# Message passing over sorted edges: the order of VectorE's register loads, the addresses of the sums, and 114 columns a chunk in place of 104

## The chip, the cores and the metric

The kernel runs on one core of a Trainium2 chip. The metric is the device time of one execution in microseconds. The kernel before took 4946.85 us, the median of three runs (4942.31 to 4949.29). The engines are named as the profile names them: PE is TensorE (PEld its weight loads), DVE VectorE, ACT ScalarE, POOL GpSimd, SP SyncE, which here only issues DMAs.

## What is computed

One layer of a graph network, over N = 12,500 nodes of 48 features and E = 400,000 edges of 32 features, with a hidden size of 128. The edges are sorted by `dst`; `src` is random.

```python
edge_index = jnp.stack([src, dst])
h = jnp.maximum(_layernorm(x, axis=-1), 0.0)
# in the layer, on h:
x_i = x[dst]
x_j = x[src]
tmp = jnp.concatenate([x_i, x_j, edge_attr], axis=1)
h = jax.nn.relu(tmp @ W1 + b1)
msg = h @ W2 + b2
out = jax.ops.segment_sum(msg, dst, num_segments=N_NODES)
# and last: x + out
```

## The kernel before

**Two stages.** `node_tables` (from L85) computes the layer norm and two tables in DRAM, one row of 128 numbers for each node: `tab_b` (h times the rows of W1 that meet `src`), and `tab_a` (h times the rows that meet `dst`, plus b1). After it the kernel asks whether the edges' windows fit (a flag), and for these data runs `windows` (from L204), which is nearly all of the time. The other branch, `general`, isn't run.

**A chunk.** `windows` goes over 391 chunks of 1024 edges, in 8 tiles of 128. Since `dst` is sorted, the edges of a chunk meet at most 80 neighbouring nodes (`W = 80`). For a chunk, these steps follow each other, each on its engine:

- SP loads 13 numbers into its registers and issues the loads of `rhs` (the chunk's 80 rows of `tab_a`, L347), of `lhs`'s edge features (L349) and of `row` (the chunk's `dst`, L351).
- POOL gathers the rows of `tab_b` for the chunk's tiles, one indirect DMA for each tile of 128 edges (L358), into one of six buffers `gb`. So the gathers of chunk c wait until the hid add of chunk c − 6 has read its buffer.
- DVE makes `lhs`'s one-hot part from `row` (L366, which also gives the degrees `deg`) and the one-hot matrix `hot` (L372).
- PE multiplies `lhs` with `rhs` into `pre` (L384); DVE adds the gathered rows, `hid = pre + gb` (L403; called the hid add here); ACT takes the relu (L408).
- PE multiplies the hidden rows with `hot`, which sums over the edges of each node (L416), and the degrees by an identity matrix (L419), into `p_g`; DVE adds `p_g` to a running sum `seg`, at a place that the chunk's first node gives (L426; the seg add).

Every 12 chunks the sums are multiplied with W2 (L452, L453), added to x (L454) and stored (L458); while it awaits that, SP issues nothing else. Then the other of two `seg` buffers is cleared and begun (L442, L444).

**Tiles without a gather.** For some chunks one of the eight tiles isn't gathered by POOL. For 305 of them (`BYCOLS`), its 128 source rows are collected as columns: `tab_b` lies transposed in SBUF too (`bt`, 128 x 12,544), and DVE and ACT copy one column after another into a tile `gt` (L339), which PE transposes into `pre` (L394); its relu is a small one of ACT (L407). For 36 others (`BYROWS`), SP loads row after row from DRAM, 12 a chunk (`gs`, L292). Each column's number has to be in a register of the engine that copies it. `load` (with `numbers`) loads the registers of one part by one instruction, `columns` makes the copies. `PARTS` says, for each part, whether it is DVE's, its first column, its length, and where its numbers lie in the table `last`:

```python
PARTS = ((True, 0, 27, 1), (True, 27, 17, 28), (False, 44, 28, 48), (False, 72, 32, 76))
PART = sum(n for _, _, n, _ in PARTS)
```

So 104 columns are copied in each chunk, 44 by DVE and 60 by ACT, whichever tile they belong to; a longer list of columns a chunk gives more tiles by columns (`tiles_of`) and so fewer gathers.

**What sets the order.** The order on each engine is the order of the code (`manual_schedule`). The loop's iteration c does the early steps of chunk c, PE's and the hid add of chunk c − 1, and the seg add of chunk c − 2. On DVE an iteration is: lhs (L366), load of part 1, hot (L372), columns of parts 0 and 1, the hid add of c − 1 (L403), the seg add of c − 2 (L426), load of the next chunk's part 0. On ACT it is: columns of part 2, relu of c − 1, columns of part 3. The place of the seg add and the row of `rhs` are numbers of a node, from which a register calculation makes the address; a column's number is already an address, since it is made in advance, for the whole table `last`, by a multiplication with 4 and an offset of `BT0`, the address at which `bt` lies.

**The start.** The three tiles `deg` are cleared by POOL (L251) inside `windows`, behind a pool's storage that `node_tables` used; so POOL's first gather, which is behind them on its engine, waits as well.

Of the kernel before, what the change touches and what calls it, by code (L numbers as in the profile page):

```python
# [8 lines left out]
F32 = mybir.dt.float32  # L9
I32 = mybir.dt.int32  # L10
AF = mybir.ActivationFunctionType
ALU = mybir.AluOpType
# [4 lines left out]
P = 128  # L17
N, D, DE, HID, E = 12500, 48, 32, 128, 400000
# [6 lines left out]
NCH = (NT + T - 1) // T  # L25
W = 80
# [4 lines left out]
L = 1024  # L31
FAR = L - W
# [11 lines left out]
U8 = mybir.dt.uint8  # L44
# [6 lines left out]
ROWS0 = 3  # L51
END = NT // T

PARTS = ((True, 0, 27, 1), (True, 27, 17, 28), (False, 44, 28, 48), (False, 72, 32, 76))
PART = sum(n for _, _, n, _ in PARTS)
BASE = 108
RPART = 12

BT0 = 16512


SEG, NEXT, SEG2 = 122, 123, 124
WIDTH = 128
SLOTS = (NCH + 2 + P - 1) // P
MOST = 32

# [137 lines left out]
def windows(nc, tc, gp, bt, ident, idx, x_t, tab_a, tab_b, dst, edge_t, w1, w2s, b2s, out_t):  # L204


    srci, rel, bw, wrow, last = idx
    with ExitStack() as es:
        one = es.enter_context(tc.tile_pool(name="wone", bufs=1))
        ld = es.enter_context(tc.tile_pool(name="ld", bufs=3))  # L210
        gtp = es.enter_context(tc.tile_pool(name="gtp", bufs=3))
# [18 lines left out]
        rows_at = slice(BASE + 1, BASE + 1 + RPART)  # L230
# [3 lines left out]
        tab8 = tab_b.rearrange("n h -> (n h)").bitcast(U8)  # L234

        place = PARTS[0][3] - 1
        for a, b in ((place, SEG2), (NEXT, SEG)):
# [5 lines left out]
        segs = []  # L243
        for k in range(2):
            seg = one.tile([P, 2, L], F32, name=f"seg{k}")
            nc.vector.memset(seg, 0.0)
            segs.append(seg)
        degs = []
        for k in range(3):
            deg = one.tile([W, P], F32, name=f"deg{k}")  # L250
            nc.gpsimd.memset(deg, 0.0)  # L251
            degs.append(deg)

        rhss = []
        for k in range(3):
            rhs = one.tile([P, HID], F32, name=f"rhs{k}")
            nc.sync.dma_start(rhs[W:K, :], w1[2 * D :, :])
            rhss.append(rhs)
        st = {}
        gts = {}  # L260
        gss = {}

        def group(c):

            return divmod(c + OFF, GQ)
# [15 lines left out]
        def node(n):  # L281
            return n.with_bounds(min_val=0, max_val=N - 1)
# [34 lines left out]
        def load(c, part):  # L317

            dve, first, n, at = PARTS[part]
            n = max(0, min(n, len(BYCOLS) * P - ((c - COLS) * PART + first))) if c >= COLS else 0  # L320
            engine = mybir.EngineType.DVE if dve else mybir.EngineType.Activation
            if part == 0 and 2 <= c < NCH + 2:
                base, *nodes = numbers(c, at - 1, n + 1, engine)
                st[c - 2]["base"] = base.with_bounds(min_val=0, max_val=FAR)
            else:
                nodes = numbers(c, at, n, engine) if n else []
            regs[c, part] = nodes

        def columns(c, part):

            dve, first, _, _ = PARTS[part]
            copy = nc.vector.tensor_copy if dve else nc.scalar.copy
            for k, at in enumerate(regs.pop((c, part), [])):
                j, e = divmod((c - COLS) * PART + first + k, P)
                of = BYCOLS[j]
                if of not in gts:
                    gts[of] = gtp.tile([HID, P], F32, name="gt")
                at = at.with_bounds(min_val=BT0, max_val=BT0 + 4 * (N - 1)) - BT0
                copy(gts[of].bitcast(U8)[:, 4 * e : 4 * e + 4], bt8[:, bass.ds(at, 4)])  # L339

        def prepare(c):
            n = min(T, NT - c * T)
            at = c * CE
            m = max(0, min(RPART, len(BYROWS) * P - (c - ROWS0) * RPART)) if c >= ROWS0 else 0
            base, *nodes = numbers(c, BASE, 1 + m, mybir.EngineType.SP)
            rhs = rhss[c % 3]
            nc.sync.dma_start(rhs[:W, :], tab_a[bass.ds(node(base), W), :])  # L347
            lhs = ld.tile([P, CE], F32, name="lhs")
            nc.sync.dma_start(lhs[W:K, : n * P], edge_t[:, at : at + n * P])  # L349
            row = ld.tile([W, CE], I16, name="row")  # L350
            nc.sync.dma_start(  # L351
                row[:, : n * P],
                dst[at : at + n * P].rearrange("(o e) -> o e", o=1).to_broadcast([W, n * P]),
            )
            st[c] = dict(n=n, rows=nodes)
            gb = gp.tile([P, T, HID], F32, name="gb")
            for t in range(n - (c in BYCOLS) - (c in BYROWS)):
                nc.gpsimd.indirect_dma_start(  # L358
                    out=gb[:, t, :], out_offset=None, in_=tab_b[:, :],
                    in_offset=bass.IndirectOffsetOnAxis(  # L360
                        ap=srci[:, c * T + t : c * T + t + 1], axis=0
                    ),
                )

            deg = degs[c % 3]
            nc.vector.tensor_scalar(  # L366
                lhs[:W, : n * P], row[:, : n * P], bw[:, c : c + 1], None,
                op0=ALU.is_equal, op1=ALU.add, accum_out=deg[:, :1],
            )
            load(c, 1)  # L370
            hot = wp.tile([P, T, W], F32, name="hot")
            nc.vector.tensor_tensor(  # L372
                hot[:, :n, :], wnum.unsqueeze(1).to_broadcast([P, n, W]),
                rel[:, c * T : c * T + n].unsqueeze(2).to_broadcast([P, n, W]), op=ALU.is_equal,
            )
            st[c].update(rhs=rhs, lhs=lhs, gb=gb, deg=deg, hot=hot)

        def before(c):
# [43 lines left out]
        def add(c):  # L422

            s = st.pop(c)
            to = segs[group(c)[0] % 2][:, :, bass.ds(s["base"], W)]
            nc.vector.tensor_add(to, to, s["p_g"])  # L426

        xs = {}
# [31 lines left out]
        with tc.manual_schedule():  # L460
            for c in range(NCH + 2):
                if c < NCH:
                    prepare(c)
                    if c < BUILD:
                        part = turn_load(c)
                    rows(c, st[c].pop("rows"))
                columns(c, 0)
                columns(c, 1)
                if 0 <= c - 1 < NCH:
                    before(c - 1)  # L470
                if 0 <= c - 2 < NCH:
                    fold(c - 2)
                if 0 <= c - 1 < NCH:
                    turned(c - 1)

                g, k = group(c - 2)
                if k == GQ - 3 or c == NCH - 1:
                    segment_load(g)
                if g > 0 and k < L // BLK:
                    segment_sum(g - 1, k, BLK)  # L480
                if g > 0 and k == STORE:
                    segment_store(g - 1, L)
                columns(c, 2)
# [145 lines left out]
def tile_gnn_preln(  # L629
# [43 lines left out]
    wrow = const.tile([P, W], F32, name="wrow")  # L673
# [85 lines left out]
    outside = nc.values_load(flag[:1, :1], min_val=0, max_val=1)  # L759

    with tc.If(outside == 0) as cmp:
        windows(nc, tc, gp, bt, ident, (srci, rel, bw, wrow, last), x_t, tab_a, tab_b, dst16, edge_t,
                w1, w2s, b2s, out_t)
    with cmp.Else():
        general(nc, tc, bt, ident, x_t, tab_a, tab_b, src_it, dst_it, dst, edge_t, w1, w2s, b2s,
# [71 lines left out]
```

## Time and profile before

| | |
|---|---|
| median of three runs | 4946.85 us (4942.31 to 4949.29) |
| the profiled execution | 4948.09 us, its span 4946.4 us |
| mean granted TensorE clock | 0.607 of full speed |
| busy, share of the span | PE 65%, PEld 58%, DVE 59%, ACT 58%, POOL 54% |
| instructions | 92,158 in all, DVE 18,764, ACT 23,270, POOL 2,812 |
| gathers on POOL (L358) | 2,784, busy 2654.2 us |
| column copies (L339) | DVE 16,540, ACT 22,500 |
| HBM over the span | 73 GB/s |

Times are microseconds of one profiled execution. A row of the costliest groups names line, engine, operation, output and inputs with their shapes and the number of instructions, then after the bar the busy time and the mean of one in ns, and after the next bar the engine's idle time just before these instructions with what ended most of it. "issue" stands for time in which the engine waited for nothing that the profile shows. A row of a timeline has its start, its length from first start to last end, engine, line, operation and how many equal ones follow each other, and in brackets the idle time ahead. Register loads, branches and DMA-issuing instructions don't count as busy. The slices of the page show that from 250 us on the kernel is even: each fortieth of the span looks like the next.

### The profile page before, as it was taken

How to read it: one execution, taken by the hardware profiler on the slowest of the kernel's cores; microseconds unless marked ns; L12 is line 12 of the kernel's file. 1: busy time of each engine (PE TensorE's matmuls, PEld its weight loads, DVE VectorE, ACT ScalarE, POOL GpSimd, SP SyncE). 2: the span in 40 equal slices, each digit the busy share in tenths (PEclk: the TensorE clock that was granted, in tenths of full speed). 3: DMA queues.
4: the chain of work that ended last, by engine and by line, in shares of the span. 5: the costliest groups of instructions: out<-in, count | busy, mean ns of one | idle time of the engine just before them, and what ended most of it. 6: DMA issues, size and time to landing. Idle time of an engine off the chain costs nothing. (4 is left out here: it accounts for less than half of the span.)

```text
span 4946.4 us, 92158 instructions
## 1 busy us (share of the span) xinstructions
PE 3197.2 (65%) x14504; PEld 2884.0 (58%) x14504; DVE 2942.6 (59%) x18764; ACT 2864.2 (58%) x23270; POOL 2675.9 (54%) x2812
## 2 busy tenths in 40 slices
PE   4565666666666666666666666666666666666666
PEld 3555556555555555656555555655666555555656
DVE  3255666666666666566666666666566666666665
ACT  2146666666566666566656566666566666566665
POOL 5555555555555555555555555555555555555552
PEclk7665655566666565556565666555555665666555
DMA  5422222222222222222222222222222222222221
GB/s 208 111 78 71 70 70 67 68 70 72 70 70 68 67 70 71 70 70 69 66 70 71 70 70 68 67 70 70 70 70 68 68 69 71 70 69 69 70 67 51
DMA packets 214695, 363.63 MB, mean 74 GB/s; under 512 B 70419, under 2 KB 119717, under 8 KB 212805
## 3 DMA queue, kind: packets, MB, share of 16 engines
q0 software_dynamic: 89120, 182.66, 14.4%
q1 hardware_dynamic: 124704, 174.89, 11.8%
q14 instruction: 491, 4.01, 0.3%
q8 instruction: 120, 1.97, 0.2%
q10 hardware_dynamic: 260, 0.10, 0.0%
HBM read 337.91 MB, written 22.07 MB: 73 GB/s over the span
## 5 line engine op out<-in xcount | busy, mean ns | idle before, releaser
L358 POOL DMA_INDIRECT gb<-tab_b,srci x2784 | 2654.2, 953 | 2167.6 <-DVE seg L426 1273.1
L339 ACT COPY gt<-bt 128x4 uint8 x22500 | 2421.0, 189 | 1761.1 <-issue 1734.7
L339 DVE COPY gt<-bt 128x4 uint8 x16540 | 1516.0, 193 | 1464.2 <-issue 1457.9
L416 PE MATMUL p_g<-hot,hid 128*128 128x80 f32 x6250 | 1368.2, 407 | 1557.6 <-ACT hid L408 1446.3
L416 PEld LDWEIGHTS p_g<-hot,hid 128*128 128x128 f32 x6250 | 1291.5, 314 | 1648.2 <-ACT hid L408 1528.5
L384 PEld LDWEIGHTS pre<-rhs,lhs 112*128 112x128 f32 x6250 | 1254.8, 306 | 140.1 <-issue 95.7
L384 PE MATMUL pre<-rhs,lhs 112*128 112x128 f32 x6250 | 1291.4, 393 | 52.1 <-DVE hid L403 38.8
L366 DVE TENSOR_SCALAR_CACHE_REDUCE lhs<-row,bw 80x1024 f32<-80x1024 int16 x391 | 498.1, 1274 | 253.5 <-issue 181.1
L403 DVE TENSOR_TENSOR hid<-pre,gb 128x896 f32<-128x896 f32 (+2 forms) x391 | 429.7, 1099 | 67.5 <-remote 53.8
L408 ACT ACTIVATE hid<-hid 128x896 f32<-128x896 f32 (+1 forms) x391 | 376.1, 962 | 120.4 <-DVE hid L403 91.1
L372 DVE TENSOR_TENSOR hot<-wnum,rel 128x640 f32<-128x640 f32 x391 | 322.0, 823 | 95.7 <-issue 95.7
L394 PE MATMUL pre<-ident,gt 128*128 128x128 f32 x610 | 220.0, 464 | 93.6 <-remote 49.8
L419 PE MATMUL p_g<-ident,deg 80*128 80x80 f32 x782 | 237.4, 405 | 2.7 <-issue 2.7
L394 PEld LDWEIGHTS pre<-ident,gt 128*128 128x128 f32 x610 | 164.0, 328 | 101.3 <-remote 53.6
L419 PEld LDWEIGHTS p_g<-ident,deg 80*128 80x128 f32 x782 | 203.4, 317 | 2.7 <-issue 2.7
L426 DVE TENSOR_TENSOR seg<-seg,p_g 128x160 f32 x391 | 120.9, 309 | 51.3 <-issue 23.4
L452 PE MATMUL p_f<-seg,w2s 128*48 128x512 f32 (+1 forms) x134 | 121.9, 1010 | 0.4 <-DVE seg L426 0.4
L407 ACT ACTIVATE hid<-pre 128x128 f32<-128x128 f32 x305 | 81.9, 268 | 60.8 <-DVE hid L403 51.7
L453 PE MATMUL p_f<-seg,b2s 1*48 1x512 f32 (+1 forms) x134 | 111.2, 924 | 0.0
L453 PEld LDWEIGHTS p_f<-seg,b2s 1*48 1x48 f32 x134 | 14.5, 159 | 102.0 <-issue 102.0
L311 ACT COPY bt<-pre 128x1024 f32<-128x1024 f32 (+1 forms) x13 | 12.4, 957 | 94.7 <-remote 71.5
L454 DVE TENSOR_TENSOR xseg<-xseg,p_f 48x512 f32<-48x512 f32 (+1 forms) x67 | 45.0, 671 | 29.7 <-PE p_f L453 22.5
(65 smaller groups left out, 348.7 us busy)
## 6 DMA issues: line engine op xcount, KB each, us to landing
gs<-tab_b SPq DMA_DIRECT2D x4608, 0.5 KB
row<-in_dst SPq DMA_DIRECT2D x390, 160.0 KB
lhs<-in_edge_t SPq DMA_DIRECT2D x390, 128.0 KB
gb<-tab_b,srci POOLq DMA_INDIRECT x2784
rhs<-tab_a SPq DMA_DIRECT2D x391, 40.0 KB
xseg<-in_x_t SPq DMA_DIRECT2D x33, 192.0 KB
out_x<-xseg SPq DMA_DIRECT2D x33, 192.0 KB
hid<-tab_b SPq DMA_DIRECT2D x12, 512.0 KB
```

What stands on the lines that cost most here:

```text
L339: copy(gts[of].bitcast(U8)[:, 4 * e : 4 * e + 4], bt8[:, bass.ds(at, 4)])
L358: nc.gpsimd.indirect_dma_start(out=gb[:, t, :], out_offset=None, in_=tab_b[:, :], in_offset=bass.IndirectOffsetOnAxis(ap=srci[:, c * T + t ...
L366: nc.vector.tensor_scalar(lhs[:W, : n * P], row[:, : n * P], bw[:, c : c + 1], None, op0=ALU.is_equal, op1=ALU.add, accum_out=deg[:, :1],)
L372: nc.vector.tensor_tensor(hot[:, :n, :], wnum.unsqueeze(1).to_broadcast([P, n, W]), rel[:, c * T : c * T + n].unsqueeze(2).to_broadcast([P ...
L384: nc.tensor.matmul(pre[:, t, :], s["lhs"][:K, t * P : (t + 1) * P], s["rhs"][:K, :], start=True, stop=c not in BYCOLS or t < n - 1,)
L394: nc.tensor.matmul(s["pre"][:, s["n"] - 1, :], gts.pop(c), ident, start=False, stop=True)
L403: nc.vector.tensor_add(h[:, :g, :], pre[:, :g, :], s["gb"][:, :g, :])
L408: nc.scalar.activation(h[:, :m, :], h[:, :m, :], AF.Relu)
L416: nc.tensor.matmul(p_g[:, 0, :], s["h"][:, t, :], s["hot"][:, t, :], start=t == 0, stop=t == n - 1)
L419: nc.tensor.matmul(p_g[:, 1, :], s["deg"], ident[:W, :W], start=True, stop=True)
L452: nc.tensor.matmul(p_f[:, :n], w2s, seg[:, 0, s], start=True, stop=False)
L453: nc.tensor.matmul(p_f[:, :n], b2s[:1, :], seg[:1, 1, s], start=False, stop=True)
```

## The change

The change has five parts.

- **Columns.** A chunk copies 114 columns, 54 by DVE (24 + 18 + 12) and 60 by ACT (28 + 32, as before). The table's rows grow from 128 to 136 numbers. The tiles by columns become 334 in place of 305, the gathers 2755 in place of 2784.
- **Order of the loads.** DVE's registers come in three loads, of 25 (one is the seg add's place), 18 and 12. The first, for the next chunk, is issued right behind the hid add and ahead of the seg add; the second behind lhs (L366), with 24 copies behind it; the third behind hot (L372), which now comes after those 24 copies; then the other 18 + 12 copies.
- **Places as addresses.** The seg add's place and the row of `rhs` stand in the table as byte addresses, so that neither needs a register calculation: `segs` lie in a pool of their own, at the address `SEG0`.
- **Form of the copies.** A column is copied as one fp32 number in a partition in place of four bytes.
- **Cleared tiles.** The three `deg` tiles are allotted and cleared (POOL) with the constants, ahead of `node_tables`.

```diff
-PARTS = ((True, 0, 27, 1), (True, 27, 17, 28), (False, 44, 28, 48), (False, 72, 32, 76))
+PARTS = (
+    (True, 0, 24, 1), (True, 24, 18, 25), (True, 42, 12, 43),
+    (False, 54, 28, 56), (False, 82, 32, 84),
+)
...
+SEG0 = 123360
+SEG_SIZE = 8 * L
...
+        seg = es.enter_context(tc.tile_pool(name="segs", bufs=1))
+
+        segs = [seg.tile([P, 2, L], F32, name=f"seg{k}") for k in range(2)]
...
+        at_place = slice(place, place + 1)
+        nc.vector.scalar_tensor_tensor(
+            last[:, :, at_place], last[:, :, at_place], 4.0, last[:, :, PLACE0 : PLACE0 + 1],
+            op0=ALU.mult, op1=ALU.add,
+        )
...
-        degs = []
-        for k in range(3):
-            deg = one.tile([W, P], F32, name=f"deg{k}")
-            nc.gpsimd.memset(deg, 0.0)
-            degs.append(deg)
...
-                at = at.with_bounds(min_val=BT0, max_val=BT0 + 4 * (N - 1)) - BT0
-                copy(gts[of].bitcast(U8)[:, 4 * e : 4 * e + 4], bt8[:, bass.ds(at, 4)])
+                at = at.with_bounds(
+                    min_val=BT0, max_val=BT0 + 4 * (N - 1), guaranteed_mod_val=0, out_of_modulus=4
+                ) - BT0
+                copy(gts[of][:, e : e + 1], bt8[:, bass.ds(at, 4)].bitcast(F32))
...
-            nc.sync.dma_start(rhs[:W, :], tab_a[bass.ds(node(base), W), :])
+            base = base.with_bounds(min_val=0, max_val=4 * HID * (N - 1))
+            nc.sync.dma_start(
+                rhs.bitcast(U8)[:W, :],
+                taba8[bass.ds(base, 4 * HID * W)].rearrange("(w h) -> w h", w=W),
+            )
...
             load(c, 1)
+            columns(c, 0)
             hot = wp.tile([P, T, W], F32, name="hot")
...
+            load(c, 2)
             st[c].update(rhs=rhs, lhs=lhs, gb=gb, deg=deg, hot=hot)
...
-            to = segs[group(c)[0] % 2][:, :, bass.ds(s["base"], W)]
+            k = group(c)[0] % 2
+            of = SEG0 + k * SEG_SIZE
+            at = s["base"].with_bounds(
+                min_val=of, max_val=of + 4 * FAR, guaranteed_mod_val=0, out_of_modulus=4
+            ) - of
+            to = segs[k].bitcast(U8)[:, :, bass.ds(at, 4 * W)].bitcast(F32)
             nc.vector.tensor_add(to, to, s["p_g"])
...
-                columns(c, 0)
+                if c >= NCH:
+                    columns(c, 0)
                 columns(c, 1)
+                columns(c, 2)
...
-                columns(c, 2)
+                columns(c, 3)
                 if 0 <= c - 1 < NCH:
                     hidden(c - 1)
-                load(c, 3)
-                columns(c, 3)
+                load(c + 1, 0)
+                load(c, 4)
+                columns(c, 4)
                 if 0 <= c - 2 < NCH:
                     add(c - 2)
                     if k == GQ - 1:
                         segment_next(g)
-                load(c + 1, 0)
-                load(c + 1, 2)
+                load(c + 1, 3)
...
+    degs = []
+    for k in range(3):
+        deg = const.tile([W, P], F32, name=f"deg{k}")
+        nc.gpsimd.memset(deg, 0.0)
+        degs.append(deg)
     gp = ctx.enter_context(tc.tile_pool(name="gp", bufs=6))
```

More of the change, by code (lines that the diff above doesn't have):

```diff
@@ L52 @@
 END = NT // T
-PARTS = ((True, 0, 27, 1), (True, 27, 17, 28), (False, 44, 28, 48), (False, 72, 32, 76))
+PARTS = (
+    (True, 0, 24, 1), (True, 24, 18, 25), (True, 42, 12, 43),
+    (False, 54, 28, 56), (False, 82, 32, 84),
+)
 PART = sum(n for _, _, n, _ in PARTS)
-BASE = 108
+BASE = 116
 RPART = 12
 BT0 = 16512
-SEG, NEXT, SEG2 = 122, 123, 124
-WIDTH = 128
+SEG0 = 123360
+SEG_SIZE = 8 * L
+SEG, NEXT, SEG2 = 130, 131, 132
+PLACE0 = 133
+WIDTH = 136
 SLOTS = (NCH + 2 + P - 1) // P
@@ L204, in windows @@
 def windows(nc, tc, gp, bt, ident, idx, x_t, tab_a, tab_b, dst, edge_t, w1, w2s, b2s, out_t):
-    srci, rel, bw, wrow, last = idx
+    srci, rel, bw, wrow, last, degs = idx
     with ExitStack() as es:
+        seg = es.enter_context(tc.tile_pool(name="segs", bufs=1))
+        segs = [seg.tile([P, 2, L], F32, name=f"seg{k}") for k in range(2)]
         one = es.enter_context(tc.tile_pool(name="wone", bufs=1))
@@ L229, in windows @@
             )
-        rows_at = slice(BASE + 1, BASE + 1 + RPART)
+        rows_at = slice(BASE, BASE + 1 + RPART)
         nc.vector.tensor_scalar(
@@ L233, in windows @@
         )
-        tab8 = tab_b.rearrange("n h -> (n h)").bitcast(U8)
+        tab8, taba8 = (t.rearrange("n h -> (n h)").bitcast(U8) for t in (tab_b, tab_a))
         place = PARTS[0][3] - 1
@@ L241, in windows @@
             )
-        segs = []
-        for k in range(2):
-            seg = one.tile([P, 2, L], F32, name=f"seg{k}")
-            nc.vector.memset(seg, 0.0)
-            segs.append(seg)
-        degs = []
-        for k in range(3):
-            deg = one.tile([W, P], F32, name=f"deg{k}")
-            nc.gpsimd.memset(deg, 0.0)
-            degs.append(deg)
+        at_place = slice(place, place + 1)
[3 more added lines that the diff above has]
+        )
+        for seg in segs:
+            nc.vector.memset(seg, 0.0)
         rhss = []
@@ L323, in load @@
                 base, *nodes = numbers(c, at - 1, n + 1, engine)
-                st[c - 2]["base"] = base.with_bounds(min_val=0, max_val=FAR)
+                st[c - 2]["base"] = base
             else:
@@ L761, in tile_gnn_preln @@
     with tc.If(outside == 0) as cmp:
-        windows(nc, tc, gp, bt, ident, (srci, rel, bw, wrow, last), x_t, tab_a, tab_b, dst16, edge_t,
+        windows(nc, tc, gp, bt, ident, (srci, rel, bw, wrow, last, degs), x_t, tab_a, tab_b, dst16, edge_t,
                 w1, w2s, b2s, out_t)
@@ L790 @@
     numbers[2 : NCH + 2, SEG2] = seg
+    numbers[2 : NCH + 2, PLACE0] = SEG0 + of % 2 * SEG_SIZE
     numbers[:NCH, BASE] = first
```

## The prediction

> **What bounds the kernel now.** I read the page's costliest groups first.
>
> ```profile
> L358 POOL DMA_INDIRECT gb<-tab_b,srci x2784 | 2654.2, 953 | 2167.6 <-DVE seg L426 1273.1
> L339 ACT COPY gt<-bt 128x4 uint8 x22500 | 2421.0, 189 | 1761.1 <-issue 1734.7
> L339 DVE COPY gt<-bt 128x4 uint8 x16540 | 1516.0, 193 | 1464.2 <-issue 1457.9
> ```
>
> No engine is near full: POOL works 54% of the span, DVE 59%. POOL stands idle for 2168 us, mostly until DVE lets it go, and DVE stands idle for 1458 us in the middle of its column copies with nothing that the profile names as awaited ("issue"). So I went to the timeline of one steady chunk, DVE first, then POOL.
>
> ```profile
> 2510.95 1.08 DVE L403 TENSOR_TENSOR hid<-pre,gb 128x896 f32<-128x896 f32 x1
> 2511.95 0.31 DVE L426 TENSOR_TENSOR seg<-seg,p_g 128x160 f32 x1
> 2512.75 1.27 DVE L366 TENSOR_SCALAR_CACHE_REDUCE lhs<-row,bw 80x1024 f32<-80x1024 int16 x1 [0.49 <-issue]
> ...
> 2514.26 0.82 DVE L372 TENSOR_TENSOR hot<-wnum,rel 128x640 f32<-128x640 f32 x1 [0.23 <-issue]
> 2515.00 2.00 DVE L339 COPY gt<-bt 128x4 uint8 x24
> 2517.93 0.33 DVE L339 COPY gt<-bt 128x4 uint8 x2 [0.93 <-issue]
> 2519.35 0.24 DVE L339 COPY gt<-bt 128x4 uint8 x2 [1.10 <-issue]
> ...
> 2521.51 0.17 DVE L339 COPY gt<-bt 128x4 uint8 x1 [0.54 <-issue]
> 2522.23 1.02 DVE L339 COPY gt<-bt 128x4 uint8 x13 [0.54 <-issue]
> 2523.15 1.08 DVE L403 TENSOR_TENSOR hid<-pre,gb 128x896 f32<-128x896 f32 x1
> ```
>
> ```profile
> 2512.30 0.95 POOL L358 DMA_INDIRECT gb<-tab_b,srci  x1 [3.69 <-DVE seg L426]
> ...
> 2519.81 0.94 POOL L358 DMA_INDIRECT gb<-tab_b,srci  x1 [0.30 <-issue]
> ```
>
> The loop reads: the hid add (L403) ends at 2512.03; 0.27 us later POOL's seven gathers start, one per 1.25 us (that add frees the oldest of gb's six buffers); DVE meanwhile does seg add, lhs, hot and 24 copies at full pace; then, at 2517, its copies come one or two at a time with holes of 0.5 to 1.1 us; at 2522.23 the holes end and the last 13 copies run in one piece; then the next hid add. I call the time from the first gather to the end of the holes **the slow stretch**. ACT's copies and SP's DMA issues step in it too and are set free at the same instant. Its length goes with the gathers. The windows view, cut from hid's end to hid's end:
>
> ```profile
> 2511.95:2524.20 12.25, 8.05 (x36) 7.75 (x36) 7.39 (x51) 7.43 (x65) 6.62 (x7) 0.59 0.31 83
> 2598.95:2609.86 10.91, 7.13 (x34) 6.94 (x34) 7.31 (x51) 7.30 (x64) 5.68 (x6) 0.62 0.25 69
> 4891.77:4899.02 7.25, 5.68 (x30) 5.68 (x31) 6.53 (x52) 5.96 (x54) 0.00 (x0) 0.67 0.18 47
> ```
>
> (PE, PEld, DVE, ACT, POOL busy with counts.) Seven gathers make a period of 12.2 us, six 10.9, none 7.25. Without a gather, at the end of the kernel, the holes are gone:
>
> ```profile
> 4894.84 3.21 DVE L339 COPY gt<-bt 128x4 uint8 x44
> ```
>
> That gives a copy's pace: (3.21 − 0.17)/43 = 0.071 us. So a chunk costs: slow stretch (about 0.27 + 1.42 us per gather) + copies left after it (12 on average over the chunks, 12 × 0.071 = 0.86 us) + hid add 1.08. For seven: 10.2 + 0.86 + 1.08 = 12.1. Time that DVE saves before the holes is slack; what counts is **how many copies are left when the stretch ends**.
>
> Decisive is what DVE's progress in the stretch follows: a number of instructions, or the clock. Over the chunks of the trace it is a number: after hot about 25 copies run fast, whether the first starts 3.0 or 4.0 us after hid's end (the first hole moves along), and then about 7 more pass in some 5 us. By the end of the stretch 30.4 are done with six gathers, 32 with seven, 32.9 with eight.
>
> **The change, part by part.**
>
> *Columns 104 to 114 a chunk, all ten on DVE (44 to 54); ACT keeps 28 + 32.* 375 chunks copy columns before and after (16540/44, 20252/54). If the stretch still lets 32 through, 22 are left where 12 were: 10 × 0.071 = 0.71 us before each hid add, and so before POOL's release: 375 × 0.71 = **+267 us**. ACT does not take over: after the stretch it has 28 copies (2.76 us in the timeline), and hid's end then comes 22 × 0.071 + 1.08 = 2.64 us after it, so ACT's relu waits no more than now.
>
> *334 tiles by columns instead of 305.* 29 gathers fewer. A gather fewer shortens the period by 1.34 (12.25 − 10.91 above) to 1.47 us (eight to seven, over all chunks); the stretch says 1.42: 29 × 1.42 = **−41 us**. PE gets 29 matmuls L394 (0.46 us), ACT 29 small relus (0.27): 21 us if all showed; both engines are idle a third of each chunk, taken as 0.
>
> *The order on DVE.* Now: hid, seg add, lhs, hot, 27 + 17 copies. Then: hid, load of the next chunk's first 25 numbers, seg add, lhs, load of 18, 24 copies, hot, load of 12, 18 + 12 copies. The register loads are no busy time; their records take 1.91 us for 28 registers and 1.38 for 17, so 0.048 us a register and 0.57 besides: 25, 18 and 12 make 1.76, 1.43, 1.14. What they cost now is the gaps ahead of lhs and hot:
>
> ```profile
> L366 DVE TENSOR_SCALAR_CACHE_REDUCE lhs<-row,bw 80x1024 f32<-80x1024 int16 x391 | 498.1, 1274 | 253.5 <-issue 181.1
> L372 DVE TENSOR_TENSOR hot<-wnum,rel 128x640 f32<-128x640 f32 x391 | 322.0, 823 | 95.7 <-issue 95.7
> ```
>
> At most 277 us (181.1 + 95.7). The first load (1.76) will run under hid (1.08) and leave a gap of about 0.5 ahead of the seg add; the second (1.43) under lhs (1.27), the third (1.14) under hot (0.82), with gaps near 0.2 and 0.3. The three are about what the two were, and all lie before the holes: **0**. A gain, if time rather than number counts, is rival C. A rule of the Trainium skill speaks against a third load and ten registers more ("Runtime: NRT & Kernel Launch", Instruction fetch mechanics): it gives about 200 ns for each register that an engine loads. By it DVE's 55 registers would be 11 us a chunk instead of 9, longer than the slack, and +2.0 us × 375 = +750 us. The row has 0.048 us a register, 4.3 us for the three loads; I take the row.
>
> *Places as addresses.* One register calculation a chunk goes on DVE (ahead of the seg add) and one on SP (ahead of L347's rhs load). On DVE it lies before the holes: 0; as one step fewer in the stretch it might let one copy more pass, −0.071 × 375 = −27 us at the most, against at least as much the other way by the third load, which is one step more; 0. SP is not awaited often (lhs for row's DMA: 42.8 us in 11 waits): 0.
>
> *Copies as one fp32 number in place of four bytes.* 193 ns and a pace of 0.071 now; no row shows the new form. The pace could fall by some ns or rise; I keep 0.071 (±0.005 × 22 × 375 = ±40 us for the range). Here a rule speaks for the change: "SBUF — State Buffer", Who interferes with whom, says that DVE copies in a two-port mode lock the ports it shares with GpSimd and so stop GpSimd's descriptor writing. If that made the stretch, copies without such a mode would bring the period towards 7.25 + 0.71 us, 1,500 us less in all. But the trace has the stretch without any DVE copy: gathers 0.95 us long every 1.25 us, and PE, which the page lets wait for no one, stepping as well:
>
> ```profile
> 133.38 0.29 PE L416 MATMUL p_g<-hot,hid 128*128 128x80 f32 x1 [2.57 <-issue]
> 134.79 0.29 PE L416 MATMUL p_g<-hot,hid 128*128 128x80 f32 x1 [1.12 <-issue]
> ```
>
> So I count nothing for it.
>
> *POOL's cleared tiles apart.* The memset of deg now holds POOL's first gather up:
>
> ```profile
> 66.25 0.48 POOL L251 MEMSET deg<- 80x128 f32 x3 [35.52 <-ACT tab L183]
> 67.24 0.97 POOL L358 DMA_INDIRECT gb<-tab_b,srci  x1 [0.50 <-issue]
> ```
>
> Without it the gather waits for tab_b only, whose traffic ends near 50 us: up to −17 us. But then 56 gathers in a row lay their slow steps over the making of tab_a (44.6 to 66.5 us), which could lose 10 us more than is gained. I take −10, nearer to the row of the wait.
>
> **Sum**: 4948.1 + 267 − 41 − 10 = **5164 us**, against the profiled execution's own 4948.1 (span 4946.4 and 1.7 around it); the median of the runs, 4946.9, is 1.2 lower, which is nothing here.
>
> **Rivals.**
>
> *A, the sum above*, 0.50: 5080 to 5205 by the pace and by two copies more or less at the stretch's end.
>
> *B, some of the ten get through*, 0.16. Where SP stands waiting for a store, DVE's share of the stretch grows:
>
> ```profile
> 2577.39 2.22 DVE L339 COPY gt<-bt 128x4 uint8 x29
> 2580.48 0.36 DVE L339 COPY gt<-bt 128x4 uint8 x3 [0.87 <-issue]
> ```
>
> 36 to 39 are done there. With 37.5 in all chunks 16.5 are left, +4.5 × 0.071 × 375 = +120: 5017 us (4940 to 5080; the lowest quarter of it within 0.2%). For it: SP has a calculation less. Against: its 12 row DMAs stay.
>
> *C, the other side: the clock counts in the stretch*, 0.27. One mechanism: hot (0.82) and the third load's wait move from before the copies into them, and if a pause refills what DVE may issue at once, then 24 copies run before hot and some 18 after it, and 42 are done by the end. Then 12 are left as now, and the gathers and the start alone count: 4948 − 51 = 4897 us (4875 to 4937). It decides from 13.9 copies left downwards, since 51 us are 1.9 × 0.071 × 375. For it: a gap of 0.23 us to 0.5 lies now before the 25 fast ones, and longer stretches let more through. Against: the start of the copies moved by 1 us changed nothing in their number.
>
> *D, worse than the sum*, 0.07: the third load counts as a step or two of the stretch and 24 are left: +53 more, 5217 us (5205 to 5260).
>
> The change does what it says, but if the stretch were set by the copies themselves it would grow on top; with 56 gathers at the start taking the same 1.41 us each, I give that no case.
>
> **Numbers.** A measurement tells about 0.2% (10 us) from no change. Faster: C, 0.27. Same: a quarter of B, 0.04. Slower: the rest, 0.69. The range reaches from C to the top of A, 4885 to 5210; A alone has 5080 to 5205.
>
> **What would show it.** In the changed profile: 20,252 DVE copies at a pace of 0.071; 2755 gathers, still 1.25 us apart; with seven gathers a period of 12.8 us and a last piece of some 22 copies ahead of L403 (A), 16 (B) or 12 (C); POOL's idle ahead of the chunk's first gather near 4.4 instead of 3.7 us; gaps "issue" ahead of seg, and hardly any ahead of lhs; first gather near 50 us. The forecast is wrong if the last piece is 14 or shorter, or if the holes are gone.

## The result, and the profile after

| | before | after |
|---|---|---|
| median of four runs | 4945.22 us (4942.31 to 4949.29) | 5213.81 us (5211.84 to 5216.07) |
| ratio | | 1.0543, 95% interval 1.0524 to 1.0561 |
| the profiled execution (its span) | 4948.09 (4946.4) | 5213.26 (5211.5) |
| DVE, ACT, POOL busy | 59%, 58%, 54% | 54%, 55%, 50% |

The change made the kernel 5.4% slower. The forecast, 5164, has the direction right and most of the size; its range ended at 5210, 4 us short. But a good part of the loss has another cause than the forecast gave it.

The costliest groups of the changed kernel, rows that answer to those of before (lines have moved: gathers L369, copies L346, lhs L377, hot L384, seg add L444, hid add L416):

```profile
L369 POOL DMA_INDIRECT gb<-tab_b,srci x2755 | 2606.3, 946 | 2509.5 <-DVE hid L416 1563.5
L346 DVE COPY gt<-bt 128x1 f32 x20252 | 1370.6, 145 | 1770.9 <-issue 1729.9
L377 DVE TENSOR_SCALAR_CACHE_REDUCE lhs<-row,bw 80x1024 f32<-80x1024 int16 x391 | 495.8, 1268 | 65.6 <-DMA row<-in_dst 62.1
L384 DVE TENSOR_TENSOR hot<-wnum,rel 128x640 f32<-128x640 f32 x391 | 321.4, 822 | 143.5 <-issue 139.9
```

The copies have become shorter (145 ns in place of 193), the gap ahead of lhs is all but gone (181 us of "issue" before, 3.5 now; the other 62 wait for the DMA of `row`), and yet DVE's unexplained idle time ahead of copies is larger than before (1730 us against 1458), and POOL waits longer for the hid add. The timeline of a chunk with seven gathers shows where. DVE:

```profile
2506.21 1.08 DVE L416 TENSOR_TENSOR hid<-pre,gb 128x896 f32<-128x896 f32 x1
2508.01 0.32 DVE L444 TENSOR_TENSOR seg<-seg,p_g 128x160 f32 x1 [0.72 <-DVE hid L416]
2508.25 1.27 DVE L377 TENSOR_SCALAR_CACHE_REDUCE lhs<-row,bw 80x1024 f32<-80x1024 int16 x1
...
2512.43 1.55 DVE L346 COPY gt<-bt 128x1 f32 x24 [2.90 <-issue]
2514.69 0.82 DVE L384 TENSOR_TENSOR hot<-wnum,rel 128x640 f32<-128x640 f32 x1 [0.71 <-issue]
2516.26 0.34 DVE L346 COPY gt<-bt 128x1 f32 x4 [0.75 <-issue]
2517.51 1.67 DVE L346 COPY gt<-bt 128x1 f32 x26 [0.91 <-issue]
2519.09 1.08 DVE L416 TENSOR_TENSOR hid<-pre,gb 128x896 f32<-128x896 f32 x1
```

and POOL's first gathers of two chunks:

```profile
2507.56 0.94 POOL L369 DMA_INDIRECT gb<-tab_b,srci  x1 [4.49 <-DVE hid L416]
...
2520.44 0.94 POOL L369 DMA_INDIRECT gb<-tab_b,srci  x1 [4.45 <-DVE hid L416]
```

The slow stretch is as long as before: it ends at 2517.51, 10.2 us after hid's end at 2507.29. But only 28 of 54 copies are done by then, and 26 are left, not the 22 forecast. And there is a hole of 2.90 us ahead of the first 24 copies, which nothing in the forecast explains. The view of the register loads' line, narrowed to one load at a time, gives its cause: the chunk's second load (18 numbers) and its third (12), and below them the second load of the kernel before (17), each with its shortest, median and longest ns:

```profile
L279 DVEq TENSOR_LOAD <-last x1: 4209/4209/4209, 2508.1 to 2508.1; - x1
...
L279 DVEq TENSOR_LOAD <-last x1: 2836/2836/2836, 2513.3 to 2513.3; - x1
```

```profile
L274 DVEq TENSOR_LOAD <-last x1: 1358/1358/1358, 2512.8 to 2512.8; - x1
```

18 numbers take 4.21 us where 17 took 1.36, and 12 take 2.84 (over all chunks the medians are 4.16, 1.38 and 2.80). The first load, of 25, takes 1.91, as the 28 did before.

### The profile page after: what moved, and what is told of

Read it like the earlier page. It is cut to its first block, busy times and chain, and to the rows that moved or that the text cites. A ratio compares the mean times of both kernels' runs of the same rounds, so it can differ in the third digit from the quotient of the medians.

```text
span 5211.5 us, 95497 instructions
## 1 busy us (share of the span) xinstructions
PE 3253.0 (62%) x14562; PEld 2934.8 (56%) x14562; DVE 2821.0 (54%) x22478; ACT 2850.0 (55%) x23299; POOL 2627.9 (50%) x2783
## 4 chain that ended last, share of the span: by engine, by line
DVE 41%; issue 41%; DVEq 9%; ACT 2%; PE 1%; SPq 1%; ACTq 1%; DMA 0%; another core or an unknown queue 0%
DVE gt L346 25%; DVEq L279 9%; DVE hid L416 7%; DVE hot L384 6%; DVE seg L444 2%; ACT gt L346 1%; DVE lhs L377 1%; ACTq L279 1%; DVE xseg L472 1%; PE p_g L429 1%; SPq L297 0%; PE pre L397 0%; PE p_f L470 0%; ACT hid L420 0%
## 5 line engine op out<-in xcount | busy, mean ns | idle before, releaser
L369 POOL DMA_INDIRECT gb<-tab_b,srci x2755 | 2606.3, 946 | 2509.5 <-DVE hid L416 1563.5
L346 ACT COPY gt<-bt 128x1 f32 x22500 | 2373.8, 187 | 1889.8 <-issue 1871.3
L429 PE MATMUL p_g<-hot,hid 128*128 128x80 f32 x6250 | 1394.3, 414 | 1753.6 <-ACT hid L421 1247.1
L429 PEld LDWEIGHTS p_g<-hot,hid 128*128 128x128 f32 x6250 | 1314.6, 319 | 1844.7 <-ACT hid L421 1344.6
L346 DVE COPY gt<-bt 128x1 f32 x20252 | 1370.6, 145 | 1770.9 <-issue 1729.9
L377 DVE TENSOR_SCALAR_CACHE_REDUCE lhs<-row,bw 80x1024 f32<-80x1024 int16 x391 | 495.8, 1268 | 65.6 <-DMA row<-in_dst 62.1
L416 DVE TENSOR_TENSOR hid<-pre,gb 128x896 f32<-128x896 f32 (+2 forms) x391 | 424.8, 1086 | 20.9 <-remote 14.7
L384 DVE TENSOR_TENSOR hot<-wnum,rel 128x640 f32<-128x640 f32 x391 | 321.4, 822 | 143.5 <-issue 139.9
L407 PE MATMUL pre<-ident,gt 128*128 128x128 f32 x668 | 240.5, 464 | 98.4 <-remote 83.8
L444 DVE TENSOR_TENSOR seg<-seg,p_g 128x160 f32 x391 | 125.8, 322 | 272.5 <-DVE hid L416 202.2
L407 PEld LDWEIGHTS pre<-ident,gt 128*128 128x128 f32 x668 | 180.3, 330 | 105.4 <-remote 89.6
L420 ACT ACTIVATE hid<-pre 128x128 f32<-128x128 f32 x334 | 92.5, 277 | 187.5 <-DVE hid L416 142.3
L460 DVE MEMSET seg<- 128x944 f32 x64 | 54.1, 845 | 9.3
```

The source lines that it names most:

```text
L346: copy(gts[of][:, e : e + 1], bt8[:, bass.ds(at, 4)].bitcast(F32))
L369: nc.gpsimd.indirect_dma_start(out=gb[:, t, :], out_offset=None, in_=tab_b[:, :], in_offset=bass.IndirectOffsetOnAxis(ap=srci[:, c * T + t ...
L377: nc.vector.tensor_scalar(lhs[:W, : n * P], row[:, : n * P], bw[:, c : c + 1], None, op0=ALU.is_equal, op1=ALU.add, accum_out=deg[:, :1],)
L384: nc.vector.tensor_tensor(hot[:, :n, :], wnum.unsqueeze(1).to_broadcast([P, n, W]), rel[:, c * T : c * T + n].unsqueeze(2).to_broadcast([P ...
L407: nc.tensor.matmul(s["pre"][:, s["n"] - 1, :], gts.pop(c), ident, start=False, stop=True)
L416: nc.vector.tensor_add(h[:, :g, :], pre[:, :g, :], s["gb"][:, :g, :])
```

## The experiments

**What the chips do.** The runs came in six groups, each on one chip with the kernel before beside it, and each ratio is taken within its group. This matters, since the chips stood in one of two conditions, whatever the kernel. In three groups the kernel before took 4949 to 5002 us, much as for the result; in the other three it took 3578 or 3579, and no trace from there has the slow stretch: POOL's gathers run on at 1.25 us each and the copies come in nearly whole pieces. One chip was met in both conditions. I write *with the stretch* and *without it*. This was not foreseen; it means that the same change has two answers.

**Where the numbers lie.** The changed kernel's second and third parts start at numbers 25 and 43 of the table's row, bytes 100 and 172. All parts of the kernel before start at multiples of 16 bytes. The *aligned kernel* is the change with that mended, nothing else (`SEG0` follows the table's size):

```diff
-    (True, 0, 24, 1), (True, 24, 18, 25), (True, 42, 12, 43),
-    (False, 54, 28, 56), (False, 82, 32, 84),
+    (True, 0, 24, 1), (True, 24, 18, 28), (True, 42, 12, 48),
+    (False, 54, 28, 60), (False, 82, 32, 88),
...
-BASE = 116
+BASE = 120
...
-SEG0 = 123360
+SEG0 = 123488
...
-SEG, NEXT, SEG2 = 130, 131, 132
-PLACE0 = 133
-WIDTH = 136
+SEG, NEXT, SEG2 = 134, 135, 136
+PLACE0 = 137
+WIDTH = 144
```

> The changed kernel with one edit: in the table of numbers, each part starts at a multiple of four numbers (16 bytes): DVE's parts at 1 (read from 0), 28 and 48 in place of 1 (0), 25 and 43. Theory 1 (the load is slow because its numbers start off a 16-byte bound): DVE's load of 18 takes 1.4 us in place of 4.2, that of 12 takes 1.1 in place of 2.8, the gap of 2.9 us ahead of the first 24 copies is about 0.2, some 32 of 54 copies are done by the end of the slow stretch in place of 28, and the time is 5077 us (5000 to 5130): 4948 + 375 x (22 x 0.061 - 12 x 0.071) - 41 - 10. Theory 2 (the place in the order: a load that runs while the gathers are under way is slow, wherever its numbers lie): both loads stay at 4.2 and 2.8, time 5214. Theory 3 (the loads are mended and time, not number, counts in the stretch): 12 left, under 4930.

Measured, without the stretch: 3529.07 against 3578.08 us, ratio 0.986 (0.9843 to 0.9876). This chip had no stretch, so the run could not yet split the 269 us. But its two loads took 1.60 and 0.88 us (medians) in place of 4.16 and 2.80, which is theory 1's side.

The reverse, on the kernel before: its second DVE part one number further on.

```diff
-(True, 27, 17, 28)
+(True, 27, 17, 29)
```

> The kernel before with one edit: the numbers of DVE's second part start at 29 in place of 28 (116 bytes in place of 112). Theory 1: the load of 17 takes about 3.9 us in place of 1.37, hot comes 2.5 us later. What that costs tells whether time before the holes is slack: if only the number of instructions counts, little is lost, some 3 copies more are left, +80 us (4990 to 5040); if the clock counts, all fast copies after the first 2.3 us are lost, up to 20 left more, +300 us and above. Theory 2: no change, 4947.

Measured, without the stretch: 4051.82 us, ratio 1.1327 (1.1308 to 1.1346). One constant, 28 to 29, costs 474 us. The timeline shows the load's hole ahead of hot, and the 44 copies in one piece, with no holes:

```profile
2009.16 0.82 DVE L372 TENSOR_TENSOR hot<-wnum,rel 128x640 f32<-128x640 f32 x1 [2.91 <-issue]
2009.90 3.31 DVE L339 COPY gt<-bt 128x4 uint8 x44
```

The load takes 3.8 to 4.1 us (1.38 before). So theory 1 holds: what makes a load slow is where its numbers lie; its place in the order is unchanged here. The rest of this expectation, on slack before the holes, could not be read where there are no holes.

The new order, addresses and form of the copies without the added columns:

> The changed kernel with aligned parts and 44 columns on DVE (20 + 12 + 12) as before, so 305 tiles by columns and 2784 gathers. It holds the new order, places as addresses, fp32 copies and the early clearing alone. Theory 1 with the count of copies as what decides: 12 left at 0.061 us, 4948 - 375 x 12 x 0.010 - 10 = 4893 us (4860 to 4940). If the new order itself costs (hot and its gap now in the stretch): 16 to 22 left, 4990 to 5100. Theory 2: the load of the second part stays slow (some 2.8 us), 5000 or more.

```diff
-    (True, 0, 24, 1), (True, 24, 18, 28), (True, 42, 12, 48),
-    (False, 54, 28, 60), (False, 82, 32, 88),
+    (True, 0, 20, 1), (True, 20, 12, 28), (True, 32, 12, 48),
+    (False, 44, 28, 60), (False, 72, 32, 88),
```

Measured, without the stretch: ratio 0.997 (0.9958 to 0.9981). The new order, the addresses, the fp32 copies and the early clearing are together worth 0.3% there.

Added columns without the rest of the change:

> The kernel before with 51 columns on DVE in place of 44 (27 + 24, as many as its registers hold in two loads), so 325 tiles by columns; all parts aligned, old order, bytes copied. If the number of copies that pass in the slow stretch is fixed at 32: 19 left in place of 12, 4948 + 375 x 7 x 0.071 - 20 x 1.42 = 5106 us (5060 to 5130). If the stretch lets more through: down to 4920.

```diff
-PARTS = ((True, 0, 27, 1), (True, 27, 17, 28), (False, 44, 28, 48), (False, 72, 32, 76))
+PARTS = ((True, 0, 27, 1), (True, 27, 24, 28), (False, 51, 28, 52), (False, 79, 32, 80))
```

(The places of the table behind it move along.) Measured, without the stretch: ratio 0.9918 (0.9901 to 0.9934). Neither of the last two expectations was put to the test, since both were on the stretch.

The next group of runs had the stretch. The changed kernel itself, first:

> The changed kernel as it is, beside the kernel before on the chip that this call gets. If the kernel before takes 3578 us here (no holes among the copies, POOL's gathers back to back): the two slow loads leave gaps of 2.9 and about 1.7 us on DVE in each chunk, which makes a DVE chain of hid 1.0, gap 1.0, seg and lhs 1.5, gap 2.9, 24 copies 1.5, gap 0.7, hot 0.8, gap 0.7, 30 copies 1.9 = 11 us against POOL's 8.75: about 4300 us, ratio 1.20. If only the place of the loads in the slow stretch made them slow: as the aligned kernel, 0.986. If the kernel before takes 4945 here: 5214 again, ratio 1.054.

Measured: 5219.38 against 4948.72 us, ratio 1.0549 (1.0532 to 1.0567): the result again. Beside it, the aligned kernel with parts on 8 bytes but not on 16:

```diff
-(True, 24, 18, 28), (True, 42, 12, 48)
+(True, 24, 18, 26), (True, 42, 12, 46)
```

> The aligned kernel of the new order with the second and third DVE parts at 26 and 46 (104 and 184 bytes: on 8, but not on 16). If a load needs 16 bytes: loads of 4.2 and 2.8 us as in the changed kernel, the same time as that. If 8 are enough: loads of 1.4 and 1.1, the time of the aligned kernel, 0.986 where the kernel before takes 3578. In between (two numbers at a time): about 2.2 and 1.5.

Measured: ratio 1.0551 (1.0533 to 1.0569), loads of 4.2 and 2.8 us: 8 bytes are not enough. And the kernel before with only the clearing of `deg` moved, as the change moves it:

> The kernel before with one edit: the three deg tiles allotted and cleared with the constants. First gather near 50 us in place of 67. The prediction's step: -10 us (between -17 and +10). If the start is hidden by what follows: 0. Where POOL's gathers run back to back from end to end, the whole 17 us show.

Measured: ratio 1.0006 (0.9997 to 1.0015), no difference. The first gather did start at 50.6 us:

```profile
50.63 0.95 POOL L353 DMA_INDIRECT gb<-tab_b,srci  x1 [19.94 <-DMA tab_b<-tab]
```

but the twenty-first hid add ends 388.9 us after the span's start in both traces: the 17 us are gone by then.

Next, the aligned kernels and the changed one beside them, meant for a chip with the stretch:

> The aligned kernel (parts at 28 and 48), once more, for a chip on which the kernel before takes 4948 us and has the slow stretch. There: loads of 1.4 and 1.1 us in place of 4.2 and 2.8. If the slow loads are the whole loss: under 4948. If the loads are half of it and ten more columns the other half: 32 of 54 copies done by the stretch's end, 22 left, 5077 us (5020 to 5120). If DVE's time before the holes is slack altogether and only the number left after the stretch counts: as the changed kernel, 5200. Where the kernel before takes 3578: 3529 again.

> The aligned kernel with 44 columns on DVE, for the same chip. If the number of copies that pass in the stretch is 32: 12 left at 0.061 us, 4893 us (4860 to 4945). If hot, now behind 20 copies, takes its 0.82 us out of the stretch: up to 16 left, 4990. Where the kernel before takes 3578: 3567 again.

> The aligned kernel with 32 columns on DVE (12 + 12 + 8) and 60 on ACT, so 270 tiles by columns and 2819 gathers. If 32 copies pass in the stretch, none is left after it: against 44 columns 375 x 12 x 0.061 = 275 us are saved and 35 more gathers cost 50, which gives 4670 us where the kernel before takes 4948 (4640 to 4750). If the stretch lengthens or ACT's 28 copies behind it take DVE's place as what ends last: no faster than 44 columns, 4900. Where the kernel before takes 3578 and the gathers are the bound: 35 x 1.25 = 44 us slower than 44 columns, 3610.

> The changed kernel on the chip of these runs. Where the kernel before takes 4948: 5217 again. Where it takes 3578: two gaps on DVE in each chunk that the aligned kernel does not have, about 2.8 and 1.0 us, on a DVE that then is the bound: about 4300 us, ratio 1.20.

This chip was without the stretch: 0.9865, 0.9968, 1.0058 (1.0041 to 1.0075) for the aligned kernel with 54, 44 and 32 DVE columns, and 1.3217 (1.3195 to 1.3239) for the changed kernel, 4730 us against 3578. So there the change costs 32% and its aligned form gains 1.3%. I had expected 1.20, from 11 us a chunk; the traces have 11.85 for most chunks and 12 to 13 for those that also add or clear the sums. Of the two holes the first was as expected (2.75 us ahead of 24 copies in the chunk looked at), the second larger (1.46 ahead of 30, in place of 1.0). Between the aligned forms the step from 54 to 44 columns follows the number of gathers: 36 us for 29 (29 × 1.25 = 36). That from 44 to 32 does not quite: 32 us for 35, where 1.25 each would be 44. The chain that ended last shows the bound too. Its share by engine, in the aligned kernel and then in the changed one:

```profile
POOL 54%; issue 26%; DMA 6%; DVE 4%; PE 4%; ACT 2%; DVEq 2%; SPq 1%; ACTq 0%; POOLq 0%
```

```profile
issue 37%; DVE 35%; POOL 11%; DVEq 7%; PE 3%; DMA 3%; ACT 3%; ACTq 1%; SPq 0%; POOLq 0%
```

POOL's gathers are the bound in the first; in the second DVE and its unnamed idle time are.

Then the comparison that decides, with the stretch:

> The aligned kernel for a chip with the slow stretch (the kernel before at 4948). Slow loads the whole loss: under 4948. Loads one half, ten more columns the other: 32 of 54 done by the stretch's end, 22 left, 5077 us (5020 to 5120). All DVE time ahead of the holes slack: 5200. Where the kernel before takes 3578: 3530 once more.

Measured: 5113.77 against 5001.08 us, ratio 1.0227 (1.0210 to 1.0244). Both parts are real: the aligned kernel still loses 2.3%, and the changed one, at 1.0549 on another chip with the stretch, 3.2 points more. A chunk of the aligned kernel with seven gathers, and its loads of 18 and of 12:

```profile
2565.06 1.08 DVE L416 TENSOR_TENSOR hid<-pre,gb 128x896 f32<-128x896 f32 x1
...
2568.77 1.55 DVE L346 COPY gt<-bt 128x1 f32 x24 [0.26 <-issue]
2570.72 0.82 DVE L384 TENSOR_TENSOR hot<-wnum,rel 128x640 f32<-128x640 f32 x1 [0.39 <-issue]
...
2572.19 0.22 DVE L346 COPY gt<-bt 128x1 f32 x2 [0.58 <-issue]
...
2577.92 1.30 DVE L346 COPY gt<-bt 128x1 f32 x20 [0.57 <-issue]
2579.14 1.08 DVE L416 TENSOR_TENSOR hid<-pre,gb 128x896 f32<-128x896 f32 x1
```

```profile
L279 DVEq TENSOR_LOAD <-last x1: 1565/1565/1565, 2567.1 to 2567.1; - x1
...
L279 DVEq TENSOR_LOAD <-last x1: 855/855/855, 2569.9 to 2569.9; - x1
```

With loads of 1.57 and 0.86 us the hole of 2.90 us is 0.26. The copies in the stretch come one or two at a time as in the kernel before, and 20 are left: 21 on average over 240 such chunks, 33 done. The forecast had 22 and 32.

With the third part alone off its bound (48 to 47):

> The aligned kernel with the third part alone off its 16-byte bound (47 in place of 48, 12 numbers): its load takes 2.8 us in place of 1.1. It is issued in the middle of the 24 copies ahead of hot, so hot (0.82) and some copies cover part: where the kernel before takes 3578, a gap of 1.2 to 1.5 us ahead of the 30 copies, of which POOL's slack of 0.3 us a chunk takes little: 375 x 1.2 = 450 us, about 3980. Where it takes 4948: the load lies in the stretch before the last piece of copies; no more than the aligned kernel if that time is slack, otherwise some 2 copies more left, +50 us.

Measured: 5119.17 us, ratio 1.0234 (1.0217 to 1.0251), no different from the aligned kernel. A load of 2.8 us after the 24 copies costs nothing with the stretch: the hole that it makes takes the place of holes that were there anyway, and as many copies are done at the end (33). So by difference it is the second part's load that costs: it stands ahead of all copies. That load alone off its bound was not run with the stretch.

The ten columns taken away again, and then twelve more, with the stretch:

> The aligned kernel with 44 columns on DVE (20 + 12 + 12), for a chip with the slow stretch. 33 copies were done by its end in the aligned kernel with 54. If that number holds: 11 left in place of 21, ratio to the kernel before 0.985 to 0.992 (12 x 0.071 - 11 x 0.061 = 0.18 us a chunk saved, hid's gap of 0.2 apart). If the copies done fall with the columns (the stretch passes a share): 17 left, ratio 1.01. Where the kernel before takes 3578: 0.997 again.

Measured, with the stretch: 4962.60 against 5002.06 us, ratio 0.9923 (0.9906 to 0.9939). 35 copies were done and 9 left on average, 10 in this chunk:

```profile
2508.24 0.70 DVE L346 COPY gt<-bt 128x1 f32 x10 [0.55 <-issue]
2508.86 1.08 DVE L416 TENSOR_TENSOR hid<-pre,gb 128x896 f32<-128x896 f32 x1
```

So the ten columns alone cost 1.0227 − 0.9923 = 3.0 points, about 150 us, with the gathers they save already counted. And the traces of this kernel and the one before, on two chips, show where the new order loses part of what it gains with 44 columns: a plain chunk with seven gathers takes 11.97 us in place of 12.14, but one that also adds the sums 12.80 in place of 12.20, and one that also clears them 13.76 in place of 12.68.

> The aligned kernel with 32 columns on DVE (12 + 12 + 8), 2819 gathers, for a chip with the slow stretch. If 33 pass in the stretch: none left after it, 0.86 us a chunk less than the kernel before and 35 more gathers at 1.42 us: 375 x 0.86 - 50 = 272 us less, ratio 0.945. If ACT's 28 copies behind the stretch (2.7 us) and its relu then end last, or the hid add must wait for something else: 0.97 to 0.99. Where the kernel before takes 3578: 1.006 again.

Measured, with the stretch: 5145.54 us, ratio 1.0287 (1.0270 to 1.0304): slower, where the count of DVE's copies alone asked for 0.945. The chain that ended last names what took DVE's place, by engine:

```profile
ACT 40%; issue 30%; PE 4%; ACTq 3%; SPq 0%; DVE 0%; DVEq 0%; another core or an unknown queue 0%; DMA 0%
```

It is ACT, with its 60 copies, which step in the stretch as DVE's do (1.2 us of "issue" ahead of one copy after another there). In the changed kernel the same line has DVE at 41% and ACT at 2%. The 35 gathers more make about 50 of the 183 us between 44 and 32 columns, by 1.42 us each; that ACT makes the rest was not tested by taking columns from it. So the gain from fewer DVE columns ends somewhere between 44 and 32.

Last, what was still open: the aligned and the changed kernel side by side, and the 51 columns in the old order:

> The aligned kernel beside the changed kernel on one chip. Where the kernel before has the slow stretch: ratio 1.023 again, 21 copies left with seven gathers. Where it has not: 0.986.

> The changed kernel beside it. With the slow stretch: ratio 1.053 to 1.055 if the kernel before sets the scale of the chip, 5214 us if not; the difference to the aligned kernel is what the two loads cost, 105 to 155 us. Without it: 1.32.

> The kernel before with 51 columns on DVE (27 + 24), the old order, aligned. With the slow stretch: 32 done by its end, 19 left, 375 x 7 x 0.071 - 20 x 1.42 = +158 us, ratio 1.032 (1.02 to 1.04). If the stretch lets a share of the added ones through: 1.00 to 1.02. Without it: 0.992 again.

This chip was again without the stretch: 0.9863, 1.3207 (1.3185 to 1.3229) and 0.9927, as before. So with the stretch the aligned and the changed kernel were not run on one chip, and 51 columns in the old order were not run there at all.

## Why the prediction was right or wrong

**The bound and the slow stretch: right, for a chip that has it.** It lasts until 10.2 us after hid's end with seven gathers in both kernels, and what is left of the copies then is what the time follows. The trace could not say that the stretch comes and goes.

**Ten columns, +267 and −41 for the gathers: right in mechanism, too large.** In the aligned kernel 33 copies are done by the stretch's end and 21 left (forecast 32 and 22). With 29 gathers fewer the step from 44 to 54 columns cost 150 us in place of 226. In a plain chunk with seven gathers it cost 12.66 − 11.97 = 0.69 us, near the forecast's 0.71, but by two errors that cancel: 12 copies more are left, not ten, and a copy as one fp32 number has a pace of 0.061 us (26 in 1.67 us above: (1.67 − 0.15)/25), not 0.071. What made the step smaller is the other chunks. The 60 of 363 looked at that also add or clear the sums do not lengthen (with seven gathers 12.84 and 13.88 us with 54 columns, 12.80 and 13.76 with 44), and those with six or eight gathers lengthen by 0.44.

**The loads, costed at 0: wrong, and this is the step that failed.** The forecast said "25, 18 and 12 make 1.76, 1.43, 1.14" and "The three are about what the two were". They take 1.91, 4.21 and 2.84. The slope of 0.048 us a register came from two rows, 28 and 17 numbers, both of which start on 16 bytes; I carried it over to numbers that start at byte 100 and 172 without looking at the offsets.

The slope is not right for aligned loads either. The medians of DVE's loads, over all traces, follow a count of steps. On the bound it is a step for each full four numbers and one for each number over, about 0.26 us a step:

| numbers | 8 | 12 | 13 | 17 | 18 | 24 | 25 | 28 |
|---|---|---|---|---|---|---|---|---|
| steps | 2 | 3 | 4 | 5 | 6 | 6 | 7 | 7 |
| us | 0.61 | 0.88 | 1.12 | 1.38 | 1.60 | 1.64 | 1.89 | 1.90 |

Off the bound every number is about a step: 12 take 2.80 us, 17 take 3.94 and 18 take 4.16, 0.23 us each. So the forecast's two rows were two steps apart, not eleven registers. That a load takes four numbers at a time is read from these durations; nothing else shows it.

The rate off the bound is near the 200 ns of the Trainium skill's "Runtime: NRT & Kernel Launch", Instruction fetch mechanics, which the forecast weighed and set aside; but that page speaks of register loads from HBM, and these read SBUF, so the +750 us that the forecast worked out from it is neither borne out nor refuted here.

If all of their extra time showed, the two loads would cost (4.16 + 2.80 − 1.60 − 0.88) × 375 = 1,680 us. Without the stretch 1195 of it shows (4725 − 3530, 3.2 us a chunk). With the stretch it is little, since the hole of 2.90 us takes the place of slack and only 4 to 5 copies fewer are done (28 in place of 33): 159 us by the ratios ((1.0549 − 1.0227) × 4948), 105 by the medians (5219 against 5114, on two chips), 94 by the 363 chunks that two traces share. The kernel before differs by 52 us between these two chips, which no run explains; so the split with the stretch is known no better than that.

**The sum came near by luck.** By the ratios, compared across chips with the stretch, the change costs 272 us: the aligned kernel with 44 columns −38 (0.9923), the ten columns +150, the two loads +159. The forecast had −10 (the start), +226 and 0 for these three. It was 28 us too high on the first (there it held the copies' pace at 0.071), 76 too high on the second and 159 too low on the third, which leaves it some 55 too low. In a plain chunk with seven gathers the luck is plain to see: the 26 copies left, at 0.061 us, take 1.58 us, where the forecast had 22 at 0.071, 1.56; the period is 12.88 where it had 12.8.

**The start, −10: wrong, 0.** The gather moved to 50.5 us as forecast; nothing behind it did. What ends the start last is open.

**The rule on the ports shared by DVE and GpSimd, counted for nothing: not contradicted.** With copies of one fp32 number the stretch is as long as it was, 10.2 us; and the kernel before, its copies unchanged, has no stretch in the chips' other condition. The copies do not make it by themselves.

**The rivals.** C (time counts, 12 left) falls: in the aligned kernel, with the loads mended and hot among the copies, 21 are left. B (some get through) has no support either: 33 done against 32. D (24 left by another step counted) had nearly the number left and, with 5217 us, the time, both by luck: 26 are left because a load of 4.2 us stands ahead of the copies, not because the third load counts as a step.

## What to carry to other kernels

A cost taken from a row holds for operations of its kind; for a register load the kind includes the address, so before carrying a slope over, compare the offsets too. And a slope drawn through two rows has not been tested: a third size would have shown the steps. Put numbers that are loaded together on multiples of 16 bytes, in fours where that is free: the aligned kernel with 44 DVE columns is a little faster than the kernel before in both conditions (0.992 with the stretch, 0.997 without), the one with 54 only without the stretch (0.986). And measure a change on more than one chip when the trace shows stalls that no wait explains: the sign of this one's main step, ten more columns, depended on them.

## What the hardware showed that was not expected

- A load of DVE's registers from SBUF takes 0.23 us a number if its numbers start off a 16-byte bound (12 in 2.8 us, 17 in 3.9, 18 in 4.2). On the bound it takes about 0.26 us for each full four numbers and for each number over (12 in 0.88 us, 17 in 1.38, 18 in 1.60, 28 in 1.90). Starting on 8 bytes is no help (4.2 us for 18). Off the bound it takes as long at the end of the kernel, when no gather is under way (4.04 us for 18).
- The slow stretch, in which the engines' instructions come in steps of about 0.7 us while gathers are under way, is a condition of the chip at that time, not of the kernel: the kernel before took 4949 to 5002 us with it and 3578 without, on one chip 5002 and 3578. It does not go with the granted TensorE clock: the changed kernel had 0.60 both with it and without. Its cause is open; no run here was made to find it.
- A copy of one fp32 number in 128 partitions follows the next after 0.061 us, a copy of the same four bytes as uint8 after 0.071.
